# The scan layer of a four-layer image kernel: inputs of its first group made in the layer before, a PSUM tile of its own for the third chunk, halves and larger transfers, and the last blocks added by VectorE

## The chip, the cores and the metric

The kernel runs on one core of a Trainium2 chip. Its time is the time on the device for one execution, in microseconds (us), and lower is better. The engines are named as the profile names them: PE (TensorE matmul; PEld is its weight load), DVE (VectorE), ACT (ScalarE), POOL (GpSimd) and SP (SyncE, which here issues DMAs). Each engine runs its own instructions in order; waits on other engines and on DMAs go through semaphores.

## The reference

Eight images of 56 x 56 pixels with 192 channels go through four layers. Each layer normalizes its input by groups of channels and adds what it computes to the input. The change is about the fourth layer and its border with the third, so that is the part to see:

```python
def s6_scan(x, A, Bv, Cv, Dv, res_scale):
    dr = Dv + res_scale
    def step(h, xt):
        h = jnp.matmul(h, A) + Bv * xt
        y = Cv * h + dr * xt
        return (h, y)
    ...
def _L3_conv_ref(x, A, Bv, Cv, Dv, res_scale):
    y_h = scan of x along H (every column of pixels is a sequence)
    y_v = scan of x along W (every row of pixels is a sequence)
    diag_p = scan along the diagonal; anti_p = scan along the anti-diagonal
    return y_h + y_v + diag_map + anti_map   # diagonal results set into zeros
...
x = x + _L3_conv_ref(_gn(x), ...)
```

All is float32. `A` is 192 x 192. Every scan has 56 steps, and a step needs the state of the step before it.

## The kernel before, in words

**Tiles of the fourth layer.** The images are worked in four groups g of two. An image pair is kept in three SBUF tiles of 128 partitions, `ys[g % 2][j]` for j = 0, 1, 2: channels 0–127 of the one image, of the other, and the remaining 64 channels of both together, each with 3136 pixels on the free axis. The two sets of tiles alternate between groups. `us[g % 2]` holds the scaled inputs u = Bv * normalized x for the same pixels, with a 57th column and row that hold the diagonal and the anti-diagonal, so that the diagonal scans ride along as a 57th sequence.

**The two chains.** Chain k = 0 goes through rows of pixels (`ringh`), chain k = 1 through columns (`ringv`). Each has 224 steps, 56 for each group, one group behind the other, and keeps its last 16 states in a ring. The function `step` (L2154 on) makes one step: ten matmuls (L2174; each leaves two records, so twenty a step) multiply the last state by `A` into one PSUM tile, and DVE adds the input and writes the new state (L2180). For three chunks of 57 columns the state has 171 columns; the first matmuls work on two chunks at once (114 columns), the eight others on one chunk. For chain 1 the add is split in 114 + 57 columns, for chain 0 it is one of 171. At the first step of a group, t = 0, there is only a DVE copy of u (L2161). A list `order` fixes how steps of the two chains alternate: the column chain is ahead by 4 steps, in the last group by 12.

**Blocks.** After every eighth step of a chain `add_block` adds the eight new states to the image: ACT multiplies them by Cv (L2184 for two chunks, L2185 for the third), then POOL adds chunk by chunk (L2205 for the image, L2207 for the diagonal).

**Preparing the next group.** `prepare(g)` hangs its work on steps of the column chain in the group before: coefficients at step 36 (POOL), the inputs u of chunks 0, 1, 2 at 40, 44, 48 (ACT, L2123), `inputs_diagonal` at 49 (POOL: L2139 copies the diagonals into u, then six scalings into dx), `settle` at 53, 57, 61 (ACT, y times its residual factor, in place) and `settle_diagonal` at 62 (POOL, L2152). For group 0 all of this stands at the start of the layer, with the inputs given to ACT, DVE and POOL, one chunk each. The order on PE, DVE, ACT and POOL is the order written in the code; no scheduler changes it.

**Transfers.** `pair_dma` issues three DMAs for one image and some rows, on SP. A group is stored and loaded by pieces of eight rows: 42 DMAs each way. When the row chain has ended a group, the group is stored (L1432) and group g + 2 loaded (L1434) into the same tiles, in this order on SP. The last group is stored in pieces from the end of the column chain on.

**The border with the third layer.** The third layer works in 28 units (an image pair, one of seven strips of 448 columns). The y tiles of the fourth layer's group 0 are loaded while its last units run. Behind the last unit stand its last output (PE L1876, ACT L1884, POOL L1887), three DVE bn_stats of the strip just computed (L1906), and three more steps of the norms of the last image pair, which the fourth layer's loop calls at column steps 10, 14 and 18 (`cx.late`). In each unit `rotate` (from L1756) makes rotated copies from two loaded tiles, `bs` and `bt`; these and the results `r0`, `r1`, `rs` are in the unit's usual pools.

## Time and profile before

| what | us |
|---|---|
| median of 3 runs | 3894.32 |
| lowest and highest run | 3891.54 and 3898.09 |
| profiled execution, own time | 3894.74 |
| its span, first to last instruction | 3892.7 |
| first scan matmul of the fourth layer (L2174) starts | 3544.34 |
| last scan add (L2180) ends | 3876.78 |

The mean granted clock of TensorE was 0.988. A row of the timeline has the start, the duration, engine, line, operation, output and inputs, the shape, and how many instructions it stands for; in square brackets is the idle time of that engine before it and who ended it. Matmuls are pipelined, so that the records of a step overlap. The fourth layer is the last 350 us of the span.

### The profile page before, as it was taken

How to read it: one execution, taken by the hardware profiler on the slowest of the kernel's cores; microseconds unless marked ns; L12 is line 12 of the kernel's file. 1: busy time of each engine (PE TensorE's matmuls, PEld its weight loads, DVE VectorE, ACT ScalarE, POOL GpSimd, SP SyncE). 2: the span in 40 equal slices, each digit the busy share in tenths (PEclk: the TensorE clock that was granted, in tenths of full speed). 3: DMA queues.
4: the chain of work that ended last, by engine and by line, in shares of the span. 5: the costliest groups of instructions: out<-in, count | busy, mean ns of one | idle time of the engine just before them, and what ended most of it. 6: DMA issues, size and time to landing. Idle time of an engine off the chain costs nothing.

```text
span 3892.7 us, 115869 instructions
## 1 busy us (share of the span) xinstructions
PE 3709.0 (95%) x51036; PEld 2642.5 (68%) x51036; DVE 2419.4 (62%) x3247; ACT 1807.2 (46%) x2061; POOL 1539.2 (40%) x1344
## 2 busy tenths in 40 slices
PE   7999999999999999998999999899989999998997
PEld 5777778777777778777667667444445555556997
DVE  5647576675757676656444444766667767774654
ACT  4444454454444454443344333343445555553663
POOL 4222242323232242334433332433335444544775
PEclk9999999999999999999999999999999999998999
DMA  8865262534436263333344443656568766643333
GB/s 160 182 140 150 80 175 80 138 89 114 103 101 158 80 172 83 106 87 105 94 117 97 115 102 87 199 170 200 175 171 191 181 162 167 158 121 99 103 105 100
DMA packets 389021, 507.94 MB, mean 130 GB/s; under 512 B 175752, under 2 KB 325192, under 8 KB 387126
## 3 DMA queue, kind: packets, MB, share of 16 engines
q1 hardware_dynamic: 386022, 495.53, 49.6%
q8 instruction: 401, 6.57, 0.7%
q0 software_dynamic: 1424, 4.14, 0.4%
q10 hardware_dynamic: 1072, 0.87, 0.1%
q14 instruction: 102, 0.84, 0.1%
HBM read 344.69 MB, written 155.65 MB: 129 GB/s over the span
## 4 chain that ended last, share of the span: by engine, by line
PE 80%; DVE 5%; ACT 4%; issue 4%; SPq 3%; DMA 2%; POOL 1%; POOLq 0%; DVEq 0%; ACTq 0%
PE c L410 10%; PE h L2174 7%; PE v L1617 6%; PE c L552 5%; PE c L1126 5%; PE c L510 4%; PE o L585 4%; PE o L410 4%; PE c L1815 3%; PE c L1824 3%; PE c L1876 3%; PE kv L1677 3%; PE y L1155 3%; PE c L606 2%; PE o L510 2%
## 5 line engine op out<-in xcount | busy, mean ns | idle before, releaser
L438 POOL TENSOR_TENSOR qv<-s,s 128x392 f32<-128x392 f32 (+3 forms) x320 | 565.6, 1799 | 1170.4 <-ACT s L418 794.1
L410 PE MATMUL c<-x,wqv 64*128 64x392 f32 x2592 | 458.3, 497 | 8.4 <-ACT s L418 4.9
L410 PEld LDWEIGHTS c<-x,wqv 64*128 64x128 f32 x2592 | 244.9, 188 | 161.7 <-ACT s L418 6.2
L418 ACT ACTIVATE s<-c,bqv 128x784 f32<-128x784 f32 (+1 forms) x247 | 224.8, 913 | 223.7 <-PE c L410 215.2
L432 DVE TENSOR_TENSOR qv<-s,s 128x784 f32<-128x784 f32 (+1 forms) x160 | 258.9, 1633 | 98.6 <-ACT s L418 98.6
L552 PE MATMUL c<-x,wp 64*128 64x224 f32 x2688 | 280.6, 354 | 13.9 <-ACT s L559 6.9
L471 ACT COPY or<-c 56x1024 f32<-56x1024 f32 x183 | 183.7, 1008 | 222.7 <-DVE ol L471 220.7
L471 DVE COPY ol<-c 56x1024 f32<-56x1024 f32 x184 | 221.7, 1210 | 85.5 <-PE c L465 85.2
L552 PEld LDWEIGHTS c<-x,wp 64*128 64x128 f32 x2688 | 253.3, 188 | 18.6 <-ACT s L559 9.1
L576 DVE TENSOR_TENSOR s<-s,c 128x896 f32<-128x896 f32 x112 | 121.8, 1088 | 219.0 <-ACT s L559 202.1
L1126 PE MATMUL c<-wv,xc 128*126 128x192 f32 (+1 forms) x1792 | 248.8, 336 | 6.6 <-ACT v L1130 3.8
L1126 PEld LDWEIGHTS c<-wv,xc 128*126 128x126 f32 (+1 forms) x1792 | 218.0, 187 | 46.6 <-issue 37.6
L1628 ACT ACTIVATE vb<-sm 128x1024 f32<-128x1024 f32 (+1 forms) x100 | 103.7, 1040 | 256.7 <-issue 224.4
L2205 POOL TENSOR_TENSOR y<-y,s 128x448 f32<-128x448 f32 x168 | 185.1, 1102 | 90.8 <-ACT s L2184 90.8
L510 PE MATMUL c<-or,ol 120*64 120x56 f32 (+1 forms) x6720 | 207.7, 221 | 9.1 <-ACT or L471 5.6
L510 PEld LDWEIGHTS c<-or,ol 120*64 120x64 f32 (+1 forms) x6720 | 199.8, 133 | 24.2 <-issue 14.0
L559 ACT ACTIVATE s<-c,bp 128x448 f32<-128x448 f32 x224 | 129.9, 631 | 184.3 <-PE c L552 183.5
L1773 POOL TENSOR_TENSOR rs<-rs,sin_win 128x896 f32<-128x896 f32 x56 | 136.3, 2452 | 192.4 <-ACT rs L1762 192.4
L2174 PE MATMUL h<-ringv,am 128*64 128x57 f32 (+1 forms) x4400 | 192.2, 235 | 20.2 <-DVE ringv L2161 13.3
L1617 PE MATMUL v<-wvb,wa 128*128 128x512 f32 (+1 forms) x400 | 192.5, 614 | 4.9 <-DVE wa L49 4.9
L2174 PE MATMUL h<-ringh,am 128*64 128x57 f32 (+1 forms) x4400 | 186.7, 232 | 8.5 <-DVE ringh L2180 8.0
L1851 ACT ACTIVATE us<-c,bub 128x896 f32<-128x896 f32 x84 | 84.7, 1008 | 225.1 <-PE c L1833 141.8
(281 smaller groups left out, 7747.7 us busy)
## 6 DMA issues: line engine op xcount, KB each, us to landing
or<-tt SPq DMA_DIRECT2D x252, 196.0 KB
ol<-tt SPq DMA_DIRECT2D x252, 196.0 KB
vt<-v SPq DMA_DIRECT2D x56, 672.0 KB
v<-vb SPq DMA_DIRECT2D x96, 384.0 KB
x<-x SPq DMA_DIRECT2D x110, 168.0 KB
wqv<-in_l_w_qv SPq DMA_DIRECT2D x40, 384.0 KB
x<-in_x SPq DMA_DIRECT2D x64, 196.0 KB
x<-x SPq DMA_DIRECT2D x110, 112.0 KB
```

The costliest lines, as they stand in the source:

```text
L410: nc.tensor.matmul(ps[:, h, 0:n], wqv[q][rows, k, i, :], xn[rows, k, g * n : (g + 1) * n], start=(k == 0), stop=(k == 2),)
L418: nc.scalar.activation(t, ps[rows, :, 0:n], AF.Silu, bias=bqv[rows, j : j + 1])
L432: nc.vector.tensor_tensor(sub(qv[rows, 7 * g :, 64 + H - 1 :], (HH * 120, 2), (120, 7), (-1, H)), *(t.rearrange("p u (h w) -> p u h w", w= ...
L438: eng.tensor_tensor(sub(qv[rows, w0:, H - 1 - 7 * g - HH * u :], (120, w1 - w0), (-1, 7)), *(t[:, u].rearrange("p (h w) -> p w h", w=H)[:, ...
L471: copy(dst[:, :, :, i0 : i0 + 8], view[rows])
L510: nc.tensor.matmul(ps[u * 64 : u * 64 + m, k, v * H : (v + 1) * H], left[:, d * H : d * H + m], right[:, d * H : (d + 1) * H], start=True, ...
L552: nc.tensor.matmul(ps[:, h, u * n : (u + 1) * n], wps[j][rows, k, u, :], xn[rows, k, g * n : (g + 1) * n], start=(u == 0 and k == 0), stop ...
L585: nc.tensor.matmul(outs[q][:, h, i * n : (i + 1) * n], wo[rows, 2 * j + u, 0:CA], gated[g][rows, u, h * n : (h + 1) * n], start=(i == 0 an ...
L1126: nc.tensor.matmul(out(i, u), group(2 if part else i, u)[rows], wv[part][rows], start=(first and u == 0), stop=True, skip_group_check=True,)
L1617: nc.tensor.matmul(out, x[:, at : at + n], wt, start=(k == 0), stop=(k == 1), skip_group_check=True,)
L2174: nc.tensor.matmul(ps[sides[c], y], am[a][:, m * CB : (m + 1) * CB], old[:, x], start=(n < 2), stop=True, skip_group_check=True,)
L2205: nc.gpsimd.tensor_tensor(v, v, line[:, j], ALU.add)
```

## The change

It has six parts.

1. A method `begin` of the object that hands data to the fourth layer takes the tiles `u0` and `dx0` in SBUF space at the end of the third layer; to make place, `bs`, `bt`, `r0`, `r1` and `rs` of the third layer have a pool of their own, which is closed ahead of the last unit (`bs` and `bt` with three buffers). Coefficients, inputs, diagonals and settling of group 0 are issued within and behind the last unit of the third layer.
2. The three bn_stats of the last strip are no longer made there. The strip is loaded again from DRAM (six DMAs on SP behind the load of group 1), its bn_stats are made at column steps 68, 70, 72, and the three late norm steps at 74, 78, 82.
3. In `step`, the matmuls into the third chunk come last. For the column chain, and for the row chain in its last 12 steps, they go to a second PSUM tile `g0` or `g1` (one buffer each), and the add is split in 114 + 57 columns.
4. Inputs are made by halves of 28 rows at steps 40, 42, 44 and 48, 50, 52; `inputs_diagonal` goes to step 53, `settle` to 55, 59, 63, `settle_diagonal` to 64.
5. A load is issued in halves of 28 rows (12 DMAs), a store in 48 rows when the column chain has ended its group and 8 rows at the end of the row chain (12 DMAs), in the last group in 40 + 8 + 8 rows.
6. In the last block of each chain, chunks 0 and 1 are multiplied and added by DVE in one instruction each for image and diagonal; only chunk 2 goes through ACT and POOL.

```diff
+        self.us = [cx.tile(pool, [128, 3, H + 1, H + 1], "u0")]
+        self.dxs = [cx.tile(pool, [128, 3, 2, H], "dx0")]
...
+            if final:
+                turned.close()
+                over.begin()
+                over.coefficients(0, over.nn[0])
...
             gs.append(g1.product())
+            if final:
+                for j in range(3):
+                    over.inputs((nc.scalar, nc.vector, nc.gpsimd)[j], 0, j)
+                over.inputs_diagonal(0)
+                over.settle(nc.gpsimd, 0, 2)
...
         out(*last[0:2], out_most(last[2]), last[3])
-        do(measures)
+        for j in range(2):
+            over.settle(nc.scalar, 0, j)
+        over.settle_diagonal(0)
...
         def load(g):
-            for r in range(0, H, NB):
+            for r in range(0, H, HH):
...
-            ps = cx.tile(psc, [128, 512], f"h{k}")[:, 0 : 3 * NS]
+            apart = k == 1 or n >= N - LAST
+            ps = cx.tile(psc, [128, 512], f"h{k}")
+            pt = cx.tile(psc, [128, 512], f"g{k}", bufs=1) if apart else ps[:, 2 * NS :]
...
-            todo += [(i, 0, 2, part[i], part[2]) for i in range(2)]
             todo += [(c, 1 + i, c, part[2], part[i]) for i in range(2) for c in range(2)]
-            todo += [(i, 1 + i, 2, part[2], part[2]) for i in range(2)]
+            todo += [(i, 0, 2, part[i], part[0]) for i in range(2)]
+            todo += [(i, 1 + i, 2, part[2], part[0]) for i in range(2)]
...
-            for js in (slice(0, 2), slice(2, 3)) if k else (slice(0, 3),):
-                nc.vector.tensor_tensor(new[:, js], ps[:, js], src[:, js], ALU.add)
+            whole = slice(0, 3 - apart)
+            v = ps[:, 0 : whole.stop * NS].rearrange("p (j s) -> p j s", s=NS)
+            nc.vector.tensor_tensor(new[:, whole], v, src[:, whole], ALU.add)
+            if apart:
+                nc.vector.tensor_tensor(new[:, 2], pt[:, part[0]], src[:, 2], ALU.add)
...
+                if j < own:
+                    c = cv[:, j : j + 1]
+                    nc.vector.scalar_tensor_tensor(v, line[1][:, j], c, v, ALU.mult, ALU.add)
+                    nc.vector.scalar_tensor_tensor(d, rest[1][:, j], c, d, ALU.mult, ALU.add)
...
-                f[40 + 4 * j] = lambda j=j: inputs(nc.scalar, g, j)
-                f[53 + 4 * j] = lambda j=j: settle(nc.scalar, g, j)
-            f[49] = lambda: inputs_diagonal(g)
-            f[62] = lambda: settle_diagonal(g)
+                f[40 + 2 * j] = lambda j=j: inputs(nc.scalar, g, j, slice(0, HH))
+                f[48 + 2 * j] = lambda j=j: inputs(nc.scalar, g, j, slice(HH, H))
+                f[55 + 4 * j] = lambda j=j: settle(nc.scalar, g, j)
+            f[53] = lambda: inputs_diagonal(g)
+            f[64] = lambda: settle_diagonal(g)
...
+        behind = [
+            lambda j=j, v=v: nc.vector.bn_stats(cx.strip[:, j, 6, :], v)
+            for j, v in enumerate((strip[0][:, 0], strip[0][:, 1], strip[1]))
+        ]
+        behind = dict(zip((68, 70, 72, 74, 78, 82), behind + cx.late))
...
-                elif k == 0 and t == H - 1:
-                    store(g)
-                    if g + 2 < NG:
-                        loaded[g + 2] = load(g + 2)
+                if k == 1 and t == H - 1:
+                    stored = (H - (LAST if g == NG - 1 else LEAD)) // NB * NB
+                    store(g, slice(0, stored))
+                elif k == 0 and t >= stored:
+                    store(g, slice(stored, t + 1))
+                    stored = t + 1
+                    if t == H - 1:
+                        stored = H
+                        if g + 2 < NG:
+                            loaded[g + 2] = load(g + 2)
```

Here `HH` is 28, `NB` 8, `LAST` 12, `LEAD` 4, and `own` is 2 in the last block of a chain and 0 elsewhere.

## The prediction

> **What bounds the kernel now.** I read the page's busy shares and clock row first, then the waits of the fourth layer's matmul line, then the order of time at the three places that these point to.

> ```profile
> PE 3709.0 (95%) x51036; PEld 2642.5 (68%) x51036; DVE 2419.4 (62%) x3247; ACT 1807.2 (46%) x2061; POOL 1539.2 (40%) x1344
> PE   7999999999999999998999999899989999998997
> PEclk9999999999999999999999999999999999998999
> ```

> TensorE (PE) sets the time nearly everywhere; the fourth layer is the last three and a half of the 40 slices (97.3 us each), where its share dips at the start and the end, and where the granted clock has its one low digit. The waits of line 2174, all of that layer's scan matmuls:

> ```profile
>   DVE ringv L2161: 27.4, 4
>   DVE ringh L2180: 18.3, 34
>   DVE ringv L2180: 16.0, 30
> ```

> The 27.4 us (counted twice, matmul and weight load) are the four first steps of a group; 34 + 30 entries are steps in which only one chain runs and PE waits for VectorE's add. In the other pairs (one column step, one row step) PE is always busy: 1.352 us a pair, so a gain must come from those waits, from the clock, or from the tail. The opening in order of time:

> ```profile
> 3529.01 4.78 PE L1876 MATMUL c<-gs,wpr 128*128 128x448 f32 x12
> 3534.73 3.00 ACT L2123 ACTIVATE u<-y,co 128x3136 f32<-128x3136 f32 x1
> 3534.91 2.23 POOL L1887 TENSOR_TENSOR xa<-xa,ya 128x448 f32<-128x448 f32 x2 [18.03 <-ACT ya L1884]
> ...
> 3538.81 4.02 DVE L49 TENSOR_SCALAR u<-y,co 128x3136 f32<-128x3136 f32 x1
> ...
> 3542.99 0.90 POOL L2139 COPY u<-u 128x168 f32<-128x168 f32 x2 [1.80 <-DVE u L49]
> ...
> 3544.34 1.49 PE L2174 MATMUL h<-ringv,am 128*64 128x114 f32 x20 [10.55 <-DVE ringv L2161]
> ```

> PE stands for 10.55 us behind inputs u. POOL had been idle 18.03 us before. Then the clock, in stretches (columns: busy us of PE, PEld, DVE, ACT, POOL; granted clock; DMA share; GB/s):

> ```profile
> 3544.30:3556.00 11.70, 9.83 (x142) 9.13 (x144) 3.17 (x12) 5.89 (x2) 6.98 (x13) 0.50 0.75 221
> ...
> 3790.50:3801.50 11.00, 7.26 (x170) 6.09 (x166) 4.41 (x17) 10.65 (x7) 10.24 (x20) 1.00 0.47 130
> ```

> After the stand, PE runs 11.7 us at half clock; single steps at full clock keep it. The group boundary before the last group, and the end:

> ```profile
> 3769.67 3.01 ACT L2123 ACTIVATE u<-y,co 128x3136 f32<-128x3136 f32 x1 [8.16 <-DMA y<-x]
> 3784.33 0.88 PE L2174 MATMUL h<-ringv,am 128*64 128x114 f32 x20 [2.70 <-DVE ringv L2161]
> 3863.57 25.75 SPq L1432 DMA_DIRECT2D out<-y  x42
> 3876.44 0.34 DVE L2180 TENSOR_TENSOR ringh<-h,u 128x171 f32<-128x171 f32 x1 [0.97 <-PE h L2174]
> 3881.76 0.22 POOL L2207 TENSOR_TENSOR y<-y,s 128x8 f32<-128x8 f32 x1
> ```

> A late load costs PE 2.70 us there; after the last add of the scan (ends 3876.78) the kernel lasts 15.9 us more, to 3892.7, while SP is issuing stores until 3889.3.

> **The change part by part.** Sums are made in the profiled execution (3894.74 us, span 3892.7, so 2.0 around it; 0.42 above the median).

> 1. *First inputs made in the third layer: +15.9.* Added before the last PE matmul there: ACT 3.00 (its idle 4.44 us before 3525.93 holds it), POOL 2.96 + 0.90 + 2.7 (dx) + 2.96 (settle) + 1.1 (coefficients) = 10.6 in the 18.03 us idle, DVE 4.02 in a gap of 3.83: 0.2 us late to PE. Their data, y, landed by about 3520. ACT settles j=0,1 (3.00 each) follow the last output at 3534.84 and end by 3540.9, ahead of the first block (about 3541.6). Without this cover the ACT and DVE items would sit on the path as now. Before, (1,1) starts at 3544.34 and (1,7) at 3556.95. After, PE goes on at about 3533.8; four single steps of 1.10 (part 2) and two pairs of 1.34 bring (1,7) to 3540.9: 16.05 earlier, less the 0.2. [...] I take the trace, 15.9.

> 2. *Third chunk apart: +3.7 in pairs, +1.8 in the last group's singles.* Today a column step's add can start only when all ten matmuls are done, and the next column step's first matmul comes 115–142 ns after its predecessor instead of 99: a column step lasts 0.680, a row step 0.662. With the last four matmuls (4 × 58.5 = 234 ns) in a PSUM tile of their own, the 114-column add starts 0.23 earlier; 18 ns × some 205 pairs = 3.7. A single column step is now 1.33 (0.92 until the add starts, 0.41 until the next matmul), then 1.10: 8 × 0.23 = 1.8. The row chain keeps one add of 171 (0.34), except in its last 12 steps. The third chunk's tile exists once: its matmuls queue behind the previous 57-column add, which by the same rows ends 1.2 us after its step began, while the tile is wanted at 1.34 + 0.43. Bounds: 0 to +5 in pairs, and below nothing by rival D.

> 3. *Halves and larger transfers: +4.3 +0.5.* A load was 42 DMAs, 27–30 us of SP issue behind a store as long. With 12 each, ACT's inputs of the last boundary (8.16 us late) find their rows: starting at 3637.7 in the first boundary's frame, 9.6 MB stored and loaded at the 190 GB/s of today need 51 us, the first half less, against some 47 to the first half input and 57 to the second. Gone: 2.70 at 3784.33 and the slow clock behind it (3785.0–3789.3, steps of 1.24 and 1.13 instead of 0.67: 1.6). The three boundaries' lone steps: 3 × 0.2 = 0.5. The inputs cost ACT two halves of about 1.63 instead of 3.00, hidden by its idle half.

> 4. *inputs_diagonal at step 53: −1.8.* At step 49 it stood ahead of the block adds of (0,47) in POOL's queue (copy at 3624.04); now behind them. In the first boundary those adds then end at about 3629.4, the copy at 3630.35, DVE's ringv copy starts 3630.4 instead of 3629.37, and PE is 0.6 later, three times. Queued behind on POOL: dx (2.6), to 3633; ACT's settle waits for dx, and the scaling of block (1,55) stands behind it; it would end at 3639.2, while step (1,64), which overwrites that ring place, comes at 3640.7. So 1.5 us of slack; range 0 to −5.

> 5. *Tail: +8.0.* Two blocks by VectorE: for the column chain 2 × (0.62, the row of an equal scalar_tensor_tensor of the third layer, + 0.15) = 1.5 us ahead of the row chain's adds. Twelve row singles today take 1.315; with the 114 add first (0.69 + 0.33 = 1.02) 12 × 0.29 = 3.5 is won: the last add ends about 2 earlier, 3874.8. The last block takes 5.2 now (ACT 1.72, POOL 3 × 1.3); after, DVE 1.5 beside ACT 0.66 and POOL 1.3: 2.3, ready at 3877.1. Then six DMAs of about 0.6 issue, and 3.4 from the last issue to the end as today: 3884.1, so 8.6. The transfers ahead must be through: 40 rows of two images are 3.44 MB from 3863.5; at the 208 GB/s of today's tail (share 0.75) they and the two 0.69 MB pieces end at 3886.7, at 235 (the loads' rate near full share, 229–241) at 3884. I take 8.0, range +5 to +10. [...]

> 6. *Small.* Three bn_stats (0.63 each) leave the opening, covered in part 1, and return at steps 68–72, where DVE has 0.48 a pair free: −0.6. The three late norm steps are moved only: 0. Six reload DMAs on SP (about 3 us) stand behind load 1 and ahead of nothing until the first store: 0. POOL's coefficients no longer hold a line 1773 addition behind a DMA at 3160 (PE idle 0.63 at 3165.70): +0.6. The rotation buffers are in another pool; the third layer's own start (PE idle 15.30 at 2881.6) hangs on them: 0, ±1.

> Sum: 15.9 + 3.7 + 1.8 + 4.3 + 0.5 − 1.8 + 8.0 − 0.6 + 0.6 = +32.4. 3894.74 − 32.4 = 3862.3, in the frame of the median 3861.9: **3862**.

> **The rivals.**
> *A, the opening doesn't move:* the third layer's last unit grows by what it takes in, or the clock falls. For it: DVE's gap is already 0.2 too short, and ACT, DVE and POOL are in order. Against: PE's last twelve matmuls hang on none of them but gs at 3528. Without part 1: 3894.3 − 16.5 = **3878**.
> *B, boundaries stall:* part 4's 1.5 us of slack is used up; ACT's settles (9 us) then hold ring places. 2–3 us each, with a slow clock behind: **3870**.
> *C, the tail stays bound by writing:* stores at 200 GB/s and part 2's bubbles not gained: **3867**.
> *D, slower:* the single third-chunk tile. Each of about 216 column steps has one more wait in the middle of its matmuls, and DVE one more hand-over. If VectorE's order makes the 57-column add late, the matmul that waits holds PE and all behind it. It decides from 32.4/216 = 0.15 us a step; at 0.25, **3916**. Against: 0.5 us of room by the rows of part 2.
> *E, nothing measurable:* the gains are taken back in parts 2 to 4; the same place as D, at 0.12–0.18 a step.

> **How the numbers follow.** The main case 0.57 (own range 3857–3867), A 0.12, B 0.13, C 0.08, D 0.07, E 0.03. Low end: parts 2, 4 and 5 at their good ends, 1.3 + 1.8 + 2 beyond the sum, 3857, less 2 for the third layer's start and the boundaries' lone steps: 3855. High end: A, 3878. Faster by over 0.2% (7.8 us, about what this measurement can tell): main, A, B, C, 0.90; same 0.03; slower 0.07.

> **What would show it.** Part 1: PE's idle before the first line-2174 matmul under 1 us, clock 1.00 in the 12 us behind it. Part 2: column steps of 0.66–0.67, single ones of 1.10, and no idle of PE before a third-chunk matmul. Part 3: no ACT idle released by the load, ringv copy not late at the third boundary. Part 4: ringv copies about 1 us late, PE 0.9–1.2 idle there. Part 5: last add to end some 9 us. The prediction is wrong if the first step still waits, if column steps lengthen, or if the boundaries' idle goes beyond 2 us.

## The result and the profile after

The kernel became a little slower: 3901.19 us median (3891.61 to 3908.79, 20 runs) against 3891.40 us (3881.07 to 3898.09, 20 runs), ratio 1.0027 with a 95% interval of 1.0019 to 1.0035. The forecast was 3862 us, with a range of 3855 to 3878.

Where the first three layers end differs between executions by more than the change moves: the last matmul of the third layer ended at 3533.8 us in the profile of before and at 3528.5 in that of after. So the fourth layer is measured from there to the end of the span: **358.9 us before (3892.7 − 3533.8), 367.9 after (3896.4 − 3528.5)**. The forecast, less the 0.6 us that lies in an earlier layer, was 358.9 − 31.8 = 327.1.

The opening is what was forecast. From the order of time of the changed kernel (line 2214 is the matmul of `step`, 2220 and 2222 are its two adds):

```profile
3528.42 0.64 PE L2214 MATMUL h<-ringv,am 128*64 128x114 f32 x12
3529.52 0.65 PE L2214 MATMUL h<-ringv,am 128*64 128x114 f32 x12 [0.22 <-DVE ringv L2220]
```

PE goes from the third layer into the scan with no stand, and a single step takes 1.10 us. From the end of the third layer to step (1,7) it is 7.1 us, before 23.2. What went wrong is in the waits of line 2214 (columns: us, times):

```profile
  issue: 62.3, 26
  DVE ringh L2220: 14.6, 18
  DVE ringv L2220: 8.8, 30
  DVE ringv L2199: 2.6, 6
```

"issue" is time in which PE waited for nothing that the profile shows; matmul and weight load are both counted, so that it is some 30 us of standing. In before, the same list for its matmul line 2174 has:

```profile
  issue: 1.1, 2
```

Two of the eleven standstills of the changed kernel that last over 0.7 us, in the timeline:

```profile
3552.32 0.38 PE L2214 MATMUL h<-ringh,am 128*64 128x57 f32 x6 [4.50 <-issue]
...
3745.52 1.38 PE L2214 MATMUL h<-ringh,am 128*64 128x114 f32 x18 [3.92 <-issue]
```

They begin in the middle of a step: the six matmul records left of a row step at 3552.32 had their inputs. The eleven make 29.5 us. Stretches of the changed kernel (busy us of PE, PEld, DVE, ACT, POOL; granted clock; DMA share; GB/s):

```profile
3536.00:3560.00 24.00, 17.82 (x476) 17.33 (x472) 10.69 (x37) 7.62 (x6) 11.95 (x21) 0.93 0.97 212
3560.00:3580.00 20.00, 17.63 (x481) 17.63 (x481) 10.16 (x35) 6.35 (x6) 9.64 (x15) 0.91 0.15 31
3580.00:3600.00 20.00, 20.00 (x608) 20.00 (x606) 13.01 (x45) 13.00 (x11) 14.98 (x29) 1.00 0.02 5
3600.00:3640.00 40.00, 36.84 (x1084) 36.28 (x1082) 25.19 (x86) 31.33 (x21) 30.37 (x55) 1.00 0.42 114
3640.00:3680.00 40.00, 31.16 (x786) 30.32 (x783) 18.88 (x67) 11.22 (x12) 19.58 (x32) 0.96 0.59 133
3680.00:3720.00 40.00, 39.04 (x1160) 38.64 (x1158) 25.47 (x90) 32.13 (x23) 29.11 (x53) 1.00 0.14 42
3720.00:3760.00 40.00, 30.75 (x818) 30.00 (x816) 17.84 (x62) 15.23 (x13) 24.34 (x43) 0.91 0.85 206
```

Where loads and stores run (DMA share 0.97, 0.59, 0.85), PE is a quarter idle, and the granted clock is 0.93, 0.96 and 0.91. Between them (3580 to 3600) PE runs 608 matmul records in 20 us; before, a full stretch of that length (3760 to 3780) had 598, so the third chunk does gain. Before, the stretch of 3640 to 3680, also with loads and stores, was this:

```profile
3640.00:3680.00 40.00, 40.00 (x1190) 39.95 (x1188) 25.62 (x89) 18.35 (x16) 29.24 (x50) 1.00 0.63 178
```

The same stretch by DMA queues, before and then after (the row DMA has the busy tenths of the 16 engines in 40 slices; behind a queue's name stand packets, MB, share of the 16 engines):

```profile
DMA  6757864687729762976038650768176828568357
...
q8 instruction: 10, 0.16, 1.7%
```

```profile
DMA  6297989999999999999999972000110000000000
...
q8 instruction: 6, 0.10, 1.1%
```

Queue 8 is the key. Over the whole kernel of before the page has this row for it:

```profile
q8 instruction: 401, 6.57, 0.7%
```

Each packet has 16384 bytes. PE ran 51036 matmuls and as many weight loads; 6.57 MB over these 102072 instructions are some 64 bytes for each, so that we read queue 8 as the one that carries PE's instructions, in blocks of 256 (102072 / 256 = 399 blocks). A scan pair has 80 in 1.33 us, so that PE uses up a block in some 4.2 us. In these 40 us it got ten before, six after. The packet records of the two traces give the time from one block's start to the next, with loads running:

```
before, 3662 to 3690:   4.0  3.8  5.0  3.8  4.3  4.5 us
after,  3640 to 3665:   8.9  9.5 us
```

A block itself takes 1.0 to 1.4 us in these stretches of both kernels; it is late, not slow. PE stands until about 1.5 us after a block has come (3550.88 and 3552.32, 3655.01 and 3656.56, 3664.68 and 3666.06).

A count of PE's records ties the standstills to the blocks. Numbered through the whole trace, matmuls, weight loads and PE's 766 semaphore instructions before that point together, 86209 are done when the first standstill begins, 86465 at the second, 90561 at the third: always 193 more than a multiple of 256. In all profiles of this document together there are 57 standstills of over 0.7 us in the fourth layer that are put down to "issue", and all 57 have this remainder; a scan pair has 80 records, of which 256 is no multiple, so no order of matmuls and no PSUM tile comes round with this period. The count also tells how far ahead the blocks are. In the fed stretch of before (3560 to 3780) PE still has 119 to 268 records to run, 218 in the median, when the transfer of the next block starts: about one block is in hand.

### The profile page after: what moved, and what is told of

It is laid out like the page before. It is cut to its first block, busy times and chain, and to the rows that moved or that the text cites. A ratio compares the mean times of both kernels' runs of the same rounds, so it can differ in the third digit from the quotient of the medians.

```text
span 3896.4 us, 115837 instructions
## 1 busy us (share of the span) xinstructions
PE 3711.4 (95%) x51036; PEld 2643.8 (68%) x51036; DVE 2420.6 (62%) x3267; ACT 1806.1 (46%) x2068; POOL 1534.0 (39%) x1336
## 3 DMA queue, kind: packets, MB, share of 16 engines
q8 instruction: 401, 6.57, 0.7%
## 5 line engine op out<-in xcount | busy, mean ns | idle before, releaser
L510 PEld LDWEIGHTS c<-or,ol 120*64 120x64 f32 (+1 forms) x6720 | 200.1, 133 | 24.6 <-issue 14.5
L2214 PEld LDWEIGHTS h<-ringh,am 128*64 128x64 f32 x4304 | 170.8, 142 | 26.3 <-issue 16.8
```

Source lines behind the costliest of these rows:

```text
L510: nc.tensor.matmul(ps[u * 64 : u * 64 + m, k, v * H : (v + 1) * H], left[:, d * H : d * H + m], right[:, d * H : (d + 1) * H], start=True, ...
L2214: nc.tensor.matmul((pt if o == 2 else ps)[sides[c], y], am[a][:, o * CB : (o + 1) * CB], old[:, x], start=(m < 2 or (apart and m in (6, 7) ...
```

## The experiments

Theory T: PE stands because the blocks of its instruction stream, moved by the same DMA engines as the data, come late while the large transfers run. Rival R1: the third chunk's PSUM tile and the new order of matmuls stop PE in a way that the profile does not name (the prediction's rival D).

| kernel | loads | stores | fourth layer, us | ratio to the before run beside it |
|---|---|---|---|---|
| before | 42 DMAs | 42 | 358.9 | 1 |
| changed | 12 | 12 | 367.9 | 1.0027 (1.0019–1.0035) |
| e1 changed, small pieces | 42 | 42 | 329.5 | 0.9919 (0.9898–0.9939) |
| e2 before, large transfers | 12 | 6 | 393.3 | 1.0080 (1.0061–1.0099) |
| e3 opening alone | 42 | 42 | 341.7 | 0.9945 (0.9925–0.9964) |
| e4 changed, small loads | 42 | 12 | 339.6 | 0.9929 (0.9906–0.9953) |
| e5 changed, loads of 14 rows | 24 | 42 | 344.3 | 0.9968 (0.9957–0.9980) |
| e6 changed, spaced large loads | 12 from ACT | 42 | 352.3 | 0.9982 (0.9973–0.9991) |
| e7 mended | 42 | 42, last group large | 325.0 | 0.9905 (0.9890–0.9920) |
| e8 changed, large loads | 12 | 42 | 367.5 | 1.0011 (1.0002–1.0020) |
| e9 the same, short runs | 12 | 42 | 358.8 | 1.0008 (0.9995–1.0021) |

The lengths of the fourth layer are each from one profiled execution, the ratios from all runs. The two can differ: e1 and e4 are 10.1 us apart in the fourth layer and 1.0 us in their medians, measured together. The medians below are of several chips, whose medians of before were 3900.65 (e1 to e4), 3893.48 (e5 to e7) and 3893.11 us (e8, e9), so that only the ratios are compared.

### e1: small pieces

```diff
-            for r in range(0, H, HH):
+            for r in range(0, H, NB):
...
-            for i in range(G):
-                pair_dma(nc, xout[g * G + i], ys[g % 2], i, store=True, rows=rows)
+            for r in range(rows.start, rows.stop, NB):
+                for i in range(G):
+                    pair_dma(nc, xout[g * G + i], ys[g % 2], i, store=True, rows=slice(r, r + NB))
```

> The changed kernel, with loads and stores issued in pieces of eight rows again (42 DMAs for a group each way), all else as changed. Theory T (PE stands because the blocks of its instruction stream, fetched through the same DMA engines, are late behind the large transfers): PE's idle put down to issue in the fourth layer, 33 us in the changed kernel, falls under 3 us, half clock after the opening is gone except in the tail, and the time is some 25 us below before: ratio about 0.9935 (0.991 to 0.996). Rival R1 (the standstills come from the third chunk's own PSUM tile and the new order of the matmuls): they stay, ratio about 1.002.

Measured: 3871.11 us median, ratio 0.9919; the fourth layer 329.5 us. The waits of line 2214, and a stretch in which group 1 is loaded:

```profile
  DVE ringh L2220: 15.3, 22
  DVE ringv L2220: 8.9, 30
  issue: 2.5, 5
  DVE ringv L2199: 2.4, 4
```

```profile
3546.00:3570.00 24.00, 23.77 (x716) 23.64 (x713) 15.56 (x55) 12.50 (x10) 15.31 (x28) 1.00 0.58 165
```

"issue" goes from 62.3 to 2.5, the clock is 1.00, PE is busy in 23.77 of 24 us with a load running. The size of the transfers alone cost 38.4 us in these two profiles (367.9 − 329.5), in the ratios 1.1% or 42 us. The PSUM tile and the order of the matmuls are untouched here, so R1 falls. The late load of the last boundary (2.70 us before) is gone here too, with 42 load DMAs and the inputs by halves: no wait of ACT for a load is left.

### e2: only the large transfers, in the kernel before

The first pair of lines is in `load`, the second in `store`, which now issues all its rows at once.

```diff
-            for r in range(0, H, NB):
+            for r in range(0, H, HH):
...
-            for r in range(rows.start, rows.stop, NB):
+            for i in range(G):
```

> The kernel before, with only the transfers of the fourth layer made large: loads in halves of 28 rows (12 DMAs), stores of all their rows at once (6 DMAs). Theory T: PE stands with no releaser of the profile for some 25 to 40 us in the stretches with loads and stores, time 3915 to 3930, ratio about 1.008. Rival R1: no such standstill, the late load of the last boundary (4 us) gone, ratio about 0.999.

Measured: 3933.06 us, ratio 1.0080, fourth layer 393.3, that is 34.4 more than before. Its waits (line 2174 as before):

```profile
  issue: 65.1, 24
  DVE ringv L2161: 21.8, 2
```

The same standstills in a kernel with the one PSUM tile. The two ringv entries are the 10.55 us of the opening, counted twice; the late load of the last boundary is gone here too (2.70 us before), so the larger transfers did what the prediction costed, and some 37 us that it had not.

### e3: the opening alone

```diff
-            apart = k == 1 or n >= N - LAST
+            apart = False
...
-            own = 2 if n == N - 1 else 0
+            own = 0
```

with the adds split as before and the small pieces of e1.

> The changed kernel with small pieces, one PSUM tile and the adds of before (114 + 57 columns for the column chain, one add of 171 for the row chain), and the last blocks through ACT and POOL: the opening, the halves of the inputs and the moved bn_stats stay. Theory T: no standstill, the opening's 16 us are won and little else: ratio about 0.9955 (0.994 to 0.997). Rival R1: also 0.9955, since the PSUM tile is undone; so this run gives the size of the opening, and e1 less e3 that of the third chunk and the tail, some 5 to 9 us.

Measured: ratio 0.9945, fourth layer 341.7. So the opening, the halves of the inputs and the earlier stores bring 17.2 us (358.9 − 341.7), and the third chunk and the last blocks another 12.2 (e1), more than the 5 to 9 that were expected here, as far as two single profiles show it (the ratios give 10 us, with intervals that overlap): 22 ns in each of some 205 pairs (the median from one column step to the next is 1.327 in e1, 1.349 in e3) make 4.5, twelve lone column steps of 1.10 in place of 1.33 make 2.8, and the tail from the last column add is 4.0 shorter (28.1 against 32.1 us).

### e4: small loads, large stores

```diff
-            for r in range(0, H, HH):
+            for r in range(0, H, NB):
```

This is the load's change of e1 alone; the stores stay as changed.

> The changed kernel with small loads (42 DMAs for a group), stores large as changed. Theory T: the standstills of the opening (8.5 us there) and those behind the loads go, those within the large stores stay: some 10 us of 33, ratio between e1 and the changed kernel, about 0.997. Rival R1: all stay, ratio 1.002.

Measured: ratio 0.9929, fourth layer 339.6; "issue" 17.3. Five standstills of 0.5 to 2.1 us stay, 7.9 us in all. The ratio is below the forecast of about 0.997, and its interval overlaps that of e1: the loads carry most of the loss, the stores less than was expected. The 10.1 us to e1 in the fourth layer can be summed up: 7.4 us more of standstills, 5.1 of half clock behind them (three stretches of 3.4 us), 2.3 less in the tail with its large stores.

### e5: loads in pieces of 14 rows

```diff
-            for r in range(0, H, HH):
+            for r in range(0, H, 14):
```

with stores in small pieces. What is it in a large load that makes a block late? Two suppositions. T1: SP hands over bytes faster than the DMA engines move them, and the engines are never free. T2: a descriptor that moves a long run holds its engine long.

> The changed kernel with stores in pieces of eight rows and loads in pieces of 14 rows (24 DMAs for a group instead of 12 or 42). Theory T1 (the instruction blocks wait behind a queue that fills because SP issues bytes faster than the DMA engines move them): 24 DMAs are issued in about 15 us, still faster than 4.8 MB can move (some 20 us), so the queue still fills, only less: some 5 to 15 us of standstill, the fourth layer between 334 and 350 us (329.5 with eight rows). Rival T2 (the size of one row's packet alone counts, 3136 bytes here, 1792 and 6272 before): about half of the changed kernel's loss, 345 us or more.

Measured: 344.3 us, ratio 0.9968, "issue" 27.3; six standstills of 0.8 to 2.2 us, 10.7 in all. The DMA share in the opening's load (3536 to 3564) was 0.84, against 0.93 as changed. Half the size gives about half the loss (329.5 with 8 rows, 367.5 with 28 in e8); T1 had the range, but T2 expects the same within a microsecond.

### e6: the same large loads, spaced

```diff
-                    pair_dma(nc, xin[g * G + i], ys[g % 2], i, rows=slice(r, r + HH))
+                    pair_dma(nc, xin[g * G + i], ys[g % 2], i, rows=slice(r, r + HH), later=paced)
...
+            if k == 1 and t % 2 == 0 and t >= (6 if g == 0 else 16) and paced:
+                paced.pop(0)()
```

> The changed kernel with stores in pieces of eight rows, and the twelve large load transfers of a group issued one at a time from ACT's queue, one every second column step (about 2.7 us), beginning at column step 6 for group 1 and at step 16 for groups 2 and 3. Size and number of the transfers are those of the changed kernel, only their spacing differs. T1 (a queue that fills): standstills all but gone, the fourth layer 329 to 335 us, plus what ACT's issue costs. T2 (one large transfer is enough to hold an instruction block up): standstills of 1 to 4 us remain in those stretches, 345 us or more.

Measured: 352.3 us, ratio 0.9982, "issue" 30.8. By its numbers this spoke for T2, but the spacing did not hold: ACT, which issued the loads, stood behind the stores of the same rows and then issued two at a time. Its delay also held a norm step on DVE (5.45 us) and, behind it, PE for 4.08 us at 3648.34, which is not a wait for instructions.

```profile
3640.78 1.07 ACT L2229 ACTIVATE s<-ringh,vec 128x912 f32<-128x912 f32 x1 [9.74 <-DMA out<-y]
...
3643.89 2.45 ACTq L1490 DMA_DIRECT2D y<-x  x2
```

In group 1's load, where no store runs, the standstills were 1.17 and 2.03 us, in place of 8.5 as changed. So with the loads spaced they were 5.3 us less in that stretch, and did not go. This run does not decide between T1 and T2.

### e8 and e9: the same bytes in long and in short runs

e8 is the changed kernel with small stores. e9 adds to it:

```diff
+            if turn is not None:
+                s, d = (v.rearrange("p (a t b) -> p a t b", t=2, b=7 * H)[:, :, turn] for v in (s, d))
```

> The changed kernel with stores in pieces of eight rows, loads large as changed: 12 DMAs, each 28 whole image rows, so that one descriptor moves 6272 bytes in one run. Both theories: the standstills behind the loads stay, those of the large stores go: the fourth layer 352 to 360 us (367.9 as changed, 329.5 with all small).

> As the run beside it, 12 load DMAs of the same 28 rows' worth of bytes for a group, but each takes every second piece of seven image rows, so that one descriptor moves only 1568 bytes. Issue on SP, bytes of a DMA and total are the same; only the length of one run differs. T2 (an instruction block waits for a turn of descriptors of the data queue, so that its delay goes with the time of one descriptor): standstills behind loads go, the fourth layer 329 to 336 us, ratio about 0.992. T1 (the queue fills because 12 DMAs are issued faster than the bytes move): as the run beside it, 352 to 360 us, ratio 0.998 or more.

Measured: 3895.30 us (1.0011) and 3894.11 us (1.0008), fourth layer 367.5 and 358.8. The stretch of the opening's load, e8 and then e9:

```profile
3536.00:3564.00 28.00, 18.82 (x483) 18.34 (x480) 10.62 (x37) 7.57 (x6) 11.38 (x18) 0.90 0.92 198
```

```profile
3536.00:3564.00 28.00, 20.35 (x557) 20.04 (x554) 11.92 (x42) 8.90 (x8) 11.49 (x20) 0.94 0.94 200
```

A run of 1568 bytes took 0.12 us in e9's trace, one of 6272 bytes 0.45 in that of the changed kernel, and the blocks are still 8.6 and 9.3 us apart in e9's opening. T2 falls: the ratios do not tell the two apart, and the standstills make 25.6 us in e8 and 23.3 in e9. Of the 8.7 us between the two profiles they are only 2.3; most of the rest is half clock (23.8 us of it in e8, 13.6 in e9, before the tail), and the profiled execution of e9 was 5.6 us under its median, that of e8 1.8 over. What the bad cases share is DMA engines that are busy with hardly a gap (share 0.92 to 0.94 here, 0.84 in e5, 0.58 in e1's load). That fits T1, and so does the issue on SP: the 12 DMAs of a load, 4.8 MB, are issued in 12.4 us as changed (from 3641.43), which is 389 GB/s, and the 42 of before in 28.2 us, 171 GB/s, while the engines moved 229 GB/s at a share of 0.98. T1 is what is left; no run here shows it by itself. What holds a block up inside the DMA engines is not shown. Small stores won only 0.4 us in e8 against the changed kernel: they took 3.9 us from the standstills (29.5 to 25.6) and gave most of it back, 3.0 us, in the tail (25.9 to 28.9 us from the last column add to the end).

### e7: the mended version

```diff
-            own = 2 if n == N - 1 else 0
+            own = 2 if k == 0 and n == N - 1 else 0
...
-                f[40 + 2 * j] = lambda j=j: inputs(nc.scalar, g, j, slice(0, HH))
-                f[48 + 2 * j] = lambda j=j: inputs(nc.scalar, g, j, slice(HH, H))
-                f[55 + 4 * j] = lambda j=j: settle(nc.scalar, g, j)
-            f[53] = lambda: inputs_diagonal(g)
-            f[64] = lambda: settle_diagonal(g)
+                f[40 + 4 * j] = lambda j=j: inputs(nc.scalar, g, j)
+                f[53 + 4 * j] = lambda j=j: settle(nc.scalar, g, j)
+            f[49] = lambda: inputs_diagonal(g)
+            f[62] = lambda: settle_diagonal(g)
```

The first pair of lines is in `add_block`, the rest in `prepare`; the lines of `load` and `store` are left out here.

> The opening, the moved bn_stats, the third chunk's own PSUM tile and the early start of the stores stay; loads and stores in pieces of eight rows again, except the last group's stores, which stay large; inputs in one piece each at 40, 44, 48, the diagonal at 49, settling at 53, 57, 61 and 62 as before; only the row chain's last block is added by VectorE, the column chain's goes through ACT and POOL. No standstill of the instruction kind but perhaps in the tail; against the run with small pieces 3.5 us less in the tail, 1 to 1.5 less at the boundaries, up to 3 more if the last load is late again: the fourth layer 324 to 328 us, ratio about 0.9905.

Measured: 3855.84 us median (3855.35 to 3860.09), ratio 0.9905, fourth layer 325.0: better than both kernels, as expected. The stretch of group 1's load, at the same distance behind the third layer as above:

```profile
3541.00:3569.00 28.00, 28.00 (x848) 28.00 (x845) 18.32 (x64) 12.58 (x11) 19.33 (x32) 1.00 0.62 183
```

848 matmul records in 28 us, in place of 483 in e8. One standstill of the instruction kind is left, 1.68 us at 3676.62, which was not expected. At the last boundary ACT still waits 5.26 us for the load (8.16 before), but no wait of PE for the ringv copy is left, so that gain came without larger loads.

## Why the prediction was wrong

**The step that failed is part 3, "Halves and larger transfers: +4.3 +0.5".** It costed a transfer by when its rows land and by SP's issue, and asked who waits for the data; what denser transfers do to PE's own instruction blocks it put at nothing, without a reason. The last boundary's late load did go: no wait of ACT or DVE for it is left. But the larger transfers cost some 40 us elsewhere (the halves of the inputs stay in e1, where the loss is gone). Without that cost the sum holds: e1's 329.5, less the 2.2 us by which its tail with small stores is longer than that of the changed kernel (28.1 against 25.9 from the last column add to the end), is 327.3; forecast were 327.1. That they meet within 0.2 us is luck, since the parts below miss by up to 1.7. What is missing, 367.9 − 327.3 = 40.6 us, is the 29.5 us of standstills and, for nearly all the rest, half-speed matmuls behind them: by an estimate from the stretches with a granted clock below 1, 1.7 (3536 to 3560), 1.8, 1.6, 3.6 and 1.6 us are lost (3820 to 3860 at 0.96 is the last), 10.3 in all.

The profile of before had a line that pointed the wrong way, and one that would have told. In 3505 to 3520 the DMA engines are as busy and PE does not stand:

```profile
3505.00:3520.00 15.00, 15.00 (x181) 7.85 (x177) 4.92 (x7) 4.37 (x6) 3.33 (x3) 1.00 0.98 229
3580.00:3600.00 20.00, 19.54 (x574) 19.34 (x572) 12.14 (x42) 9.34 (x8) 12.81 (x21) 1.00 0.02 3
```

The first reads as if PE were not hurt by transfers at full share. But there it runs 358 instructions in 15 us, 24 a microsecond, so that a block lasts 10.7 us; in the scan it runs 57, and a block lasts 4.5. With about one block in hand, a block that is 5 us late is covered in the one and a standstill in the other.

One reading of the waits was wrong too, without changing a sum: the four entries of line 2161 (27.4 us) are not the four first steps of a group but two stands, 10.55 us in the opening and 2.70 at the last boundary, each counted for the matmul and for the weight load. The 34 + 30 entries are in the same way 32 steps.

**Part 1, the opening, +15.9: right.** 16.1 by the profile (7.1 in place of 23.2). The granted clock was 1.00 in the single steps of the start (3528.4 to 3533.5, PE busy 4.21 of 5.10 us), so the row of before that the prediction went by held. Behind the standstill of 4.50 us it was 0.50 from 3552.76 to 3556.17, around that of 3.92 us from 3743.91 to 3750.73: one or two stretches of 3.41 us, not the 11.7 us behind the stand of before.

**Part 2, third chunk apart, +3.7 and +1.8: right.** 1.330 us (1.327 in e1, without standstills) in place of 1.346 from column step to column step, single steps 1.10. No wait of line 2214 is for an add of 57 columns (line 2222); rival D had the sign of the whole result right by luck, since its place was wrong.

**Part 4, inputs_diagonal, −1.8: oversized.** PE waited 0.52, 0.30 and 0.30 us for the ringv copy at the three boundaries:

```profile
3615.30 0.64 PE L2214 MATMUL h<-ringv,am 128*64 128x114 f32 x12 [0.52 <-DVE ringv L2199]
```

That is 1.1 us in all; 0.6 each, 1.8, was forecast. The 1.5 us of slack in ACT's queue held.

**Part 5, tail, +8.0: 6.3.** From the last column add to the end 32.2 us before, 25.9 after. The term that was mis-sized is VectorE's block for the column chain, 1.5 us by the forecast:

```profile
3871.01 1.03 DVE L2254 SCALAR_TENSOR_TENSOR y<-ringv,vec,y 128x448 f32<-128x448 f32 x1 [0.54 <-POOL y L2257]
...
3871.96 1.06 DVE L2255 SCALAR_TENSOR_TENSOR y<-ringv,vec,y 128x8 f32<-128x8 f32 x1
...
3874.39 1.06 PE L2214 MATMUL h<-ringh,am 128*64 128x114 f32 x12 [3.59 <-DVE ringh L2220]
```

With columns of the image as operands the two of 128 x 448 elements took 1.03 and 1.00 us and not the 0.62 of the contiguous row that it was costed by. The four instructions take 3.1 us (3871.01 to 3874.08); with a wait of 0.54 us for POOL's block before them they hold the row chain for 3.59 us, and the next row steps run at a lower clock (0.50 from 3873.61 to 3880.43), four of 1.44 us and one of 1.26 in place of 1.02. The end behind the last row add made up for a part of it: 7.7 us, where some 9 were forecast. In e7, where the column block went back to ACT and POOL, this wait is gone: 24.6 us from the last column add to the end.

**The rivals.** A did not happen. B's place (the boundaries, 1.1 us) and C's (the tail, 1.7 us short of the forecast) cost little. The loss is not in any of them: all had looked for a wait on data, on an engine or on a PSUM tile.

## What to carry to other kernels

Here the DMA engines moved PE's instructions too: the page counts queue 8's 401 packets, 6.57 MB, in a share of the same 16 engines. Before making transfers larger or denser, count the instructions per microsecond of the engine that sets the time, divide a block of 256 by them (here 80 in 1.33 us, so 4.2 us a block), and ask whether a block may come later than that (here 8.6 to 10.2 us after the one before it). The slower issue of 42 DMAs left gaps in the DMA engines here (share 0.58 in e1's load), and PE was busy for 23.77 of 24 us in that stretch. And a wait that the profile puts down to "issue" in the middle of a run of like instructions is a reason to look at the instruction queue's packets in that stretch, and to see whether the standstills lie a multiple of 256 records apart.
